# A second level of Strassen's algorithm for two of seven products instead of one, in a two-layer graph kernel

## The chip, the cores and the metric

The kernel runs on one core of one Trainium2 chip. The metric is the device time of one execution in microseconds, as a median of runs. TensorE is called PE in the profile (PEld for its weight loads), VectorE DVE, ScalarE ACT, GpSimd POOL, and the queue of SyncE, which issues most transfers, SP.

## The reference

x is 64 x 256 x 512, the adjacency matrix 256 x 256 of zeros and ones, each weight 512 x 512, all float32.

```python
def layer_0(h, adj, Wq, Wk, Wv):
    q, k, v = h @ Wq.T, h @ Wk.T, h @ Wv.T            # for each of 64 graphs
    rel = adj.T * (q @ k.transpose(0, 2, 1))
    rel = rel / norm(rel, axis=2, keepdims=True)
    return rel @ v

def layer_1(h, adj, weight, bias):
    return (adj @ h) @ weight + bias

x = x + layer_0(maximum(layernorm(x), 0), adj, Wq, Wk, Wv)
x = x + layer_1(maximum(layernorm(x), 0), adj, weight, bias)
```

## The kernel before

**The work of a pair.** Two graphs form a pair, and there are 32 pairs (`NP`). Wq and Wk are merged into one matrix once, so a pair i has three projections of 512 tokens by a 512 x 512 weight: G (h by the merged matrix), V (h by Wv), and the mix (y by the weight of layer 1, added onto x). Between them stand the scores (G with h, then masked, squared, scaled and turned), attend (rel with V, added onto x) and the gather (y, the adjacency with h of layer 1, in two fp32r terms).

**Products.** Each projection, the scores and attend use the Winograd form of Strassen's algorithm: seven products of half-size blocks and sums of blocks. A product of a projection is four matmuls of 128 x 128 weights and 256 columns into one PSUM bank. The factors that are sums come from VectorE: `left_factors` (L168 to L171) and `right_operands` (L133 to L136), each a list of four steps: for the left, s0, the total (in place when it is given three rooms), s1 and s2. The seven factors of a left matrix are then 1: a(0,0), 2: a(0,1), 3: s2, 4: a(1,1), 5: the total, 6: s1, 7: s0. Products are emitted in the order 1, 5, 6, 3, 7, 2, 4; bank_a takes 1, 6, 7 and 4, bank_c 5 and 3, bank_b 2. After each product a `take` reads the bank: ScalarE copies a first block (L431 for G, L475 for V, L514 for the scores), VectorE adds (L433, L477, L516); attend (L619) and the mix (L703) always add on VectorE.

**The second level.** For pairs in the middle, product 2 is dropped and done at a second level: 7 small matmuls of 128 x 128 by 128 columns in four groups, into one bank, bank_d, in the parts at_a, at_b and at_c (L440 for G, L487 for V and mix). Group 1 is small products 1 and 5, group 2 is 6 and 3, group 3 is 7 and 2, group 4 is 4. VectorE adds each part to the result (L449, L491): five adds of 128 columns, one of 256. The small factors on the left come from `second_of_h` and `second_of_y` (four VectorE operations on 128 columns each).

**The order.** PE, DVE and ACT execute in the order in which the program emits (`manual_schedule`). A step list is run by `run_steps`, which after step n emits the other work that a dictionary `side` gives for slot n. So a side item stands on its engine behind the take of its own slot. The function `steady` emits one iteration for 28 values of i: attend of pair i beside V of pair i+1 (`attend_and_v`), scores of i+1, G of i+2, gather of i, mix of i. In it, names stand for lists of single operations:

- `totals`, `row_squares`, `mean`, `root0`, `end0`, `relus0`: LayerNorm of layer 0 by ScalarE, with small VectorE operations (L334 to L354). The result h goes through SP transfers into `blocks` (`place_blocks`, L406, 16 of them) and through VectorE transposes (`turned`, L416), and `sums` are its left factors.
- `halves`, `root`, `end`, `relus`, `uppers`, `lowers`: LayerNorm of layer 1 (L307 to L319, L651, L655); `relus` also emit the bias add on POOL (L647).
- `masks`, `squares`, `norm_root`, `inverse`, `scales`, `place`, `turns`: the scores after their products (L519 to L546); `place` is 16 SP transfers.
- `gs` are G's factors, `y_steps` the left factors of y, `y_second` the small ones; `v_steps` and `rel_steps` are the factors of V and of the turned rel for attend.

The output of a pair is one transfer on POOL's queue (L715), the input one on SP's (L88).

Of the kernel before, what the change touches and what calls it, by code (L numbers as in the profile page):

```python
# [19 lines left out]
def kernel(  # L20
# [35 lines left out]

    nc = tc.nc
    P = 128
# [18 lines left out]
    whole = ctx.enter_context(tc.tile_pool(name="whole", bufs=2))  # L77
# [3 lines left out]
    X, H, HL, G, V, R, H2, Y, HL2, Y2 = ({} for _ in range(10))  # L81
# [22 lines left out]
    warm = const.tile([P, P], F32, name="warm")  # L104
# [39 lines left out]
    def second_right(factor, name):  # L144

        t = const.tile([P, 4, P], F32, name=f"{name}_t")
        return right_operands(lambda j, k: factor[:, j, ts(k, P)], [t[:, n] for n in range(4)])

    def second_left(factor, room):

        return left_factors(lambda i, j: factor[:, j, ts(i, P)], [room[:, n] for n in range(4)])
# [52 lines left out]
    def second_level(matmul, add):  # L204

        bank = ps_m.tile([P, 512], F32, tag="pm", name="bank_d")
        at_a, at_b, at_c = (bank[:, ts(r, P)] for r in range(3))

        def group_1():
            matmul(at_a, 1, True)
            matmul(at_c, 5, False)
            add(0, 0, at_a)
            add(1, 1, at_c)

        def group_2():
            matmul(at_a, 6, False)
            matmul(at_c, 3, False)
            add(0, 1, at_a)  # L220

        def group_3():
            matmul(at_a, 7, False)
            matmul(at_b, 2, False)
            add(1, 1, at_a)
            add(0, None, bank[:, P : 3 * P])

        def group_4():
            matmul(at_a, 4, False)
            add(1, 0, at_a)  # L230

        return group_1, group_2, group_3, group_4

    def two_level_steps(product, take, matmul, add, spacer):

        one, five, six, three, seven, _, four = winograd_steps(product, take)
        groups = second_level(matmul, add)
        return [  # L240
            lambda: run([one]),
            lambda: run([five]),
            lambda: run([six, groups[0]]),
            lambda: run([three, groups[1]]),
            lambda: run([seven, groups[2]]),
            lambda: run([spacer, groups[3]] if spacer else [groups[3]]),
            lambda: run([four]),
        ]
# [76 lines left out]
    def norm_by_scalar(src, scratch):  # L325
# [5 lines left out]
        nb = small.tile([P, TC], F32, tag="nb", name="nb")  # L331

        def total(c):
            nc.scalar.activation(scratch[:, c, :], src[:, c, :], AF.Copy, accum_out=sm[:, c : c + 1])  # L334
# [4 lines left out]
        def square(c):  # L339
            nc.scalar.activation(  # L340
                scratch[:, c, :], src[:, c, :], AF.Square, bias=sm[:, c : c + 1],
                accum_out=sq[:, c : c + 1],
            )
# [9 lines left out]
        def relu(c):  # L353
            nc.scalar.activation(  # L354
                scratch[:, c, :], src[:, c, :], AF.Relu, bias=nb[:, c : c + 1], scale=rs[:, c : c + 1]
            )
# [4 lines left out]
        return each(total), mean, each(square), root, end, each(relu)  # L361
# [12 lines left out]
    def ln0_by_scalar(i):  # L374
        H[i] = work.tile([P, TC, D], F32, tag="hy", name=f"h_{i}")
        return norm_by_scalar(flat(X[i]), H[i])

    def new_ht(i):
        return twice.tile([P, DC, NC, NB * P], F32, tag="ht", name=f"ht_{i}")

    def transposes_by_matmul(i):
        h, ht = H.pop(i), new_ht(i)
        for d in range(DC):
            pt = ps_m.tile([P, T], F32, tag="pm", name="pt")
            for half in range(NC):
                for b in range(NB):
                    nc.tensor.transpose(
                        pt[:, ts(half * NB + b, P)], h[:, b * NC + half, ts(d, P)], ident
                    )
            nc.scalar.copy(ht[:, d].rearrange("p h t -> p (h t)"), pt)  # L390
        HL[i], sums = left_operands(twice, ht, "hs", i)
        return sums

    def second_of_h(i):

        room = work.tile([P, 4, P], F32, tag="hs2", name=f"hs2_{i}")
        HL2[i], steps = second_left(HL[i][2], room)
        return steps
# [11 lines left out]
    def transpose_blocks(i):  # L410

        ht = new_ht(i)
# [7 lines left out]
        HL[i], sums = left_operands(twice, ht, "hs", i)  # L420
        return [(lambda d=d, k=k: step(d, k)) for d in range(DC) for k in range(NC)], sums

    def project_g(i, side={}, second=False, spacer=None):

        g = work.tile([P, DC, NC, HT_], F32, tag="g", name=f"g_{i}")

# [8 lines left out]
        product = product_tokens_moving(HL[i], m_right)  # L435
        if not second:
            winograd(product, take, side)
        else:
            def matmul(out, n, start):
                nc.tensor.matmul(  # L440
                    out, m_second[n], HL2[i][n], start=start, stop=True, skip_group_check=True
                )

            def add(t, k, sums):
                if k is None:
                    dst, sums = g[:, 0:HC, 0, ts(t, P)], sums.rearrange("p (e t) -> p e t", e=HC)
                else:
                    dst = g[:, k, 0, ts(t, P)]
                nc.vector.tensor_add(dst, sums, dst)  # L449

            run_steps(two_level_steps(product, take, matmul, add, spacer), side)
        G[i] = g
# [31 lines left out]
    def second_weights_moving(left, right, x):  # L484

        def matmul(out, n, start):
            nc.tensor.matmul(out, left[n], right[n], start=start, stop=True, skip_group_check=True)  # L487

        def add(b, k, sums):
            dst = x[:, b, 0, 0:HD] if k is None else x[:, b, 0, ts(k, P)]  # L490
# [4 lines left out]
    def v_steps_by_two_levels(i):  # L495
        products = v_products(i)
        second = second_weights_moving(HL2.pop(i), wv_second, V[i])
        return two_level_steps(*products, *second, None)
# [124 lines left out]
    def attend_and_v(i, first_done, v_products, side):  # L623


        for at, (step, v_step) in enumerate(zip(attend_steps(i), v_products)):
            step()
            if at or not first_done:
                v_step()
            run(side.get(at, ()))  # L630


    def ln1(i, exact):
# [9 lines left out]
        def relu_bias(c):  # L643
            if exact:
                whole_h[c] = whole.tile([P, D], F32, tag="h2c", name="h2c")
# [16 lines left out]
    def gather_steps(i, exact):  # L662
# [21 lines left out]
        return [(lambda b=b, d0=d0: step(b, d0)) for b in range(NB) for d0 in range(0, DC, 2)], sums  # L684
# [6 lines left out]
    def second_of_y(i):  # L691

        room = work.tile([P, 4, P], F32, tag="ys2", name=f"ys2_{i}")
        Y2[i], steps = second_left(Y[i][2], room)
        return steps

    def mix(i, side={}, early=False, spacer=None):
        xt = X.pop(i)
        last, taken = i + 1 == NP, set()

        def take(t, k, bank, first):
            block = (slice(None), slice(None), t, slice(k * HD, (k + 1) * HD))
            nc.vector.tensor_add(xt[block], bank.rearrange("p (b e) -> p b e", b=NB), xt[block])  # L703
            if last and ((t, k) in taken or (t, k) == (1, 0)):
                nc.sync.dma_start(out=outs[i][block], in_=xt[block])
            taken.add((t, k))

        product = product_weights_moving(Y.pop(i), w_right)
        if i in Y2:
            second = second_weights_moving(Y2.pop(i), w_second, xt)  # L710
            run_steps(two_level_steps(product, take, *second, spacer), side)
        else:
            winograd(product, take, side, early)
        if not last:
            nc.gpsimd.dma_start(out=outs[i], in_=xt)  # L715
# [94 lines left out]
    m_second, m_second_steps = second_right(m_right[2], "m2")  # L810
    wv_second, wv_second_steps = second_right(wv_right[2], "wv2")
    w_second, w_second_steps = second_right(w_right[2], "w2")
# [8 lines left out]
    def pairs(exact):  # L821
        with tc.manual_schedule(engines=in_order):
            sums = first_pairs(exact)
            v_products = v_steps_by_two_levels(2)
            for i in range(1, NP - 3):
                if i + 4 < NP:
                    load(i + 4)
                sums, v_products = steady(i, exact, sums, v_products, first_done=i > 1)
            last_pairs(exact, sums, v_products)

    def first_pairs(exact):
# [35 lines left out]
            3: turned2[4:6] + relus[2:4], 4: turned2[6:8] + wv_second_steps,  # L867
            5: m_second_steps + turns[0:2], 6: turns[2:4],
# [3 lines left out]
            0: sums2[0:1], 1: sums2[1:2], 2: sums2[2:3], 6: sums2[3:4] + w_second_steps,  # L872
        })
        stats, *parts = ln1(0, exact)
        attend(0, by_slot({c: [stats[c]] for c in range(TC)}, {
# [3 lines left out]
        if exact:  # L879
            nc.vector.tensor_copy(adjt_r, adjt_sb)  # L880
        project_g(2, by_slot(layer_1(parts), {
            1: [inverse], 3: scales + [place], 4: turned3[0:1], 5: turned3[1:2], 6: turned3[2:4],
        }))
        v_steps, rel_steps = attend_operands(1)
        h_second = second_of_h(2)
        y_steps = gather(0, exact, {0: turned3[4:6], 1: turned3[6:7], 2: turned3[7:8]})
        run(y_steps[0:2])
        mix(0, {
# [121 lines left out]
```

## Time and profile before

| | before |
|---|---|
| median of 3 runs | 1717.07 us (1716.89 to 1717.33) |
| the profiled execution, its time | 1717.26 us |
| its span, first to last instruction | 1715.2 us |
| granted TensorE clock | 0.999 |
| PE busy | 1704.2 us, 99% |
| DVE busy | 1386.5 us, 81% |
| ACT busy | 794.5 us, 46% |
| POOL busy | 192.2 us, 11% |

How to read it: busy is the part of the span in which the engine had an instruction under way; matmuls are pipelined, so a busy PE is not one at its peak. VectorE instructions overlap too: one of 512 columns has a duration of 0.68 us, and the next starts 0.60 us after it. The profile counts two instructions for each float32 matmul.

### The profile page before, as it was taken

How to read it: one execution, taken by the hardware profiler on the slowest of the kernel's cores; microseconds unless marked ns; L12 is line 12 of the kernel's file. 1: busy time of each engine (PE TensorE's matmuls, PEld its weight loads, DVE VectorE, ACT ScalarE, POOL GpSimd, SP SyncE). 2: the span in 40 equal slices, each digit the busy share in tenths (PEclk: the TensorE clock that was granted, in tenths of full speed). 3: DMA queues.
4: the chain of work that ended last, by engine and by line, in shares of the span. 5: the costliest groups of instructions: out<-in, count | busy, mean ns of one | idle time of the engine just before them, and what ended most of it. 6: DMA issues, size and time to landing. Idle time of an engine off the chain costs nothing.

```text
span 1715.2 us, 27061 instructions
## 1 busy us (share of the span) xinstructions
PE 1704.2 (99%) x9680; PEld 1523.6 (89%) x9680; DVE 1386.5 (81%) x3141; ACT 794.5 (46%) x1835; POOL 192.2 (11%) x167
## 2 busy tenths in 40 slices
PE   8999999999999999999999999999999999999998
PEld 7989988999898999889998989998899989899986
DVE  6788888888888888888888888888888888788765
ACT  3435544445445455444454354554444544545332
POOL 0011100111101111001111011110011110111111
PEclk9999999999999999999999999999999999999999
DMA  7423332233332233323333322333233333322002
GB/s 239 65 44 70 77 85 68 58 62 79 82 76 73 45 78 76 86 66 61 60 79 81 76 73 42 80 76 84 68 61 62 79 82 74 75 39 58 29 14 75
DMA packets 425984, 122.48 MB, mean 71 GB/s; under 512 B 398064, under 2 KB 399344, under 8 KB 425840
## 3 DMA queue, kind: packets, MB, share of 16 engines
q1 hardware_dynamic: 413248, 80.28, 25.1%
q0 software_dynamic: 8432, 32.51, 5.0%
q10 hardware_dynamic: 4160, 7.87, 1.4%
q8 instruction: 79, 1.29, 0.3%
q14 instruction: 65, 0.53, 0.1%
HBM read 38.27 MB, written 33.55 MB: 42 GB/s over the span
## 4 chain that ended last, share of the span: by engine, by line
PE 97%; DVE 2%; DMA 0%; ACT 0%; issue 0%; ACTq 0%; DVEq 0%
PE bank_a L276 26%; PE bank_c L276 13%; PE bank_a L264 13%; PE py L675 7%; PE bank_a L288 7%; PE bank_c L264 6%; PE bank_d L487 6%; PE bank_a L612 6%; PE bank_c L288 3%; PE bank_c L612 3%; PE bank_d L440 3%; PE bank_b L288 2%; PE bank_b L612 1%; PE bank_b L276 1%; PE pu L577 1%; DVE st L307 0%
## 5 line engine op out<-in xcount | busy, mean ns | idle before, releaser
L475 ACT COPY v<-bank_a 128x512 f32<-128x512 f32 x96 | 56.3, 587 | 459.7 <-PE bank_a L276 459.7
L647 POOL TENSOR_TENSOR x_ring<-x_ring,bias_bc 128x512 f32<-128x512 f32 x128 | 167.3, 1326 | 816.7 <-ACT h2c L319 816.7
L675 PE MATMUL py<-adjt_r,h 128*128 128x256 f32 x1024 | 137.1, 287 | 0.0
L319 ACT ACTIVATE h2c<-x_ring,nb,rs 128x512 f32<-128x512 f32 x128 | 100.6, 810 | 63.8 <-DVE h L655 45.0
L675 PEld LDWEIGHTS py<-adjt_r,h 128*128 128x128 f32 x1024 | 125.8, 189 | 1.6
L276 PE MATMUL bank_a<-w_t,ys 128*128 128x256 f32 x512 | 121.1, 379 | 0.3 <-DVE ys L170 0.3
L264 PE MATMUL bank_a<-hs,m_t 128*128 128x256 f32 x512 | 121.0, 379 | 0.0
L276 PE MATMUL bank_a<-wv_t,hs 128*128 128x256 f32 x512 | 120.9, 379 | 0.0
L703 DVE TENSOR_TENSOR x_ring<-bank_a,x_ring 128x512 f32<-128x512 f32 x128 | 88.5, 691 | 35.1 <-PE bank_a L276 35.1
L276 PEld LDWEIGHTS bank_a<-wv_t,hs 128*128 128x128 f32 x512 | 97.3, 190 | 13.2
L276 PEld LDWEIGHTS bank_a<-w_t,ys 128*128 128x128 f32 x512 | 92.9, 190 | 14.6 <-DVE ys L170 0.7
L264 PEld LDWEIGHTS bank_a<-hs,m_t 128*128 128x128 f32 x512 | 95.1, 190 | 11.8
L715 POOL DMA_DIRECT2D out_dram<-x_ring x31 | 24.0, 773 | 686.4 <-issue 501.2
L307 DVE BATCH_NORM_STATS2 st<-x_ring 128x6 f32<-128x512 f32 x144 | 96.4, 670 | 0.4
L416 DVE STREAM_TRANSPOSE ht<-blocks 128x256 f32<-128x256 f32 x248 | 93.3, 416 | 2.3 <-DMA blocks<-h 2.0
L655 DVE TENSOR_TENSOR h<-h2c,h 128x512 fp32r<-128x512 f32 x128 | 92.3, 723 | 3.0 <-ACT h L651 2.9
L334 ACT ACTIVATE h<-x_ring 128x512 f32<-128x512 f32 x112 | 69.5, 623 | 40.5 <-PE bank_a L276 40.5
L354 ACT ACTIVATE h<-x_ring,nb,rs 128x512 f32<-128x512 f32 x112 | 82.0, 802 | 12.4 <-DVE nb L351 12.4
L679 ACT COPY yt<-py 128x512 f32<-128x512 f32 x128 | 74.5, 582 | 26.1 <-PE py L675 26.1
L536 ACT ACTIVATE rel<-rel,rn 128x256 f32<-128x256 f32 x124 | 52.9, 497 | 68.5 <-DVE rn L533 68.5
L619 DVE TENSOR_TENSOR x_ring<-bank_a,x_ring 128x512 f32<-128x512 f32 x116 | 79.3, 683 | 1.0 <-PE bank_a L612 1.0
L340 ACT ACTIVATE h<-x_ring,sm 128x512 f32<-128x512 f32 x112 | 79.5, 714 | 0.0
(229 smaller groups left out, 4104.2 us busy)
## 6 DMA issues: line engine op xcount, KB each, us to landing
blocks<-h SPq DMA_DIRECT2D x496, 64.0 KB, 2.3
out_dram<-x_ring POOLq DMA_DIRECT2D x31, 1024.0 KB, 4.7
x_ring<-in_x_dram SPq DMA_DIRECT2D x28, 1024.0 KB, 5.2
placed<-rel SPq DMA_DIRECT2D x496, 32.0 KB, 2.0
x_ring<-in_x_dram ACTq DMA_DIRECT2D x4, 1024.0 KB, 5.2
wq_sb<-in_L_gnn_Wq_dram SPq DMA_DIRECT2D x4, 256.0 KB, 5.0
wk_sb<-in_L_gnn_Wk_dram ACTq DMA_DIRECT2D x4, 256.0 KB, 6.2
wv_sb<-in_L_gnn_Wv_dram ACTq DMA_DIRECT2D x1, 1024.0 KB, 5.3
```

What stands on the lines that cost most here:

```text
L264: nc.tensor.matmul(bank[:, e * HT_ : (e + 1) * HT_], right[n][:, d, ts(e, P)], left[n][:, d, :], start=(start and e == 0 and d == 0), stop ...
L276: nc.tensor.matmul(bank[:, b * HD : (b + 1) * HD], left[n][:, d, ts(b, P)], right[n][:, d, :], start=(start and b == 0 and d == 0), stop=( ...
L288: nc.tensor.matmul(bank[:, ts(b, P)], right[n][:, d, ts(b, P)], left[n][:, d, ts(b, P)], start=(start and b == 0 and d == 0), stop=(d == H ...
L307: nc.vector.bn_stats(st[:, c, :], src[:, c, :])
L319: nc.scalar.activation(dst, src[:, c, :], AF.Relu, bias=nb[:, c : c + 1], scale=rs[:, c : c + 1])
L416: nc.vector.transpose(ht[:, d, half].rearrange("p (b n) -> p b n", b=NB), by_half[:, :, half, d])
L487: nc.tensor.matmul(out, left[n], right[n], start=start, stop=True, skip_group_check=True)
L612: nc.tensor.matmul(bank[:, ts(b, HD)], left[n][:, b], right[n][:, b], start=(start and b == 0), stop=True, skip_group_check=True,)
L647: nc.gpsimd.tensor_tensor(xt[:, c, :], xt[:, c, :], bias_bc, ALU.add)
L655: nc.vector.tensor_sub(dst[:, 1, c, :], whole_h[c], dst[:, 0, c, :].bitcast(F32))
L675: nc.tensor.matmul(pm[:, d, :], left[:, b * NC + m, ts(d0 + d, P)], right, start=(n == 0), stop=(n == len(terms) - 1),)
L703: nc.vector.tensor_add(xt[block], bank.rearrange("p (b e) -> p b e", b=NB), xt[block])
```

## The change

Products 2 and 3 of each projection are both dropped and done at a second level. In one small group, the two run side by side: at_a has a bank of its own (bank_e), at_b and at_c share bank_d, and each part is twice as wide, so that one VectorE add serves both. Four pieces change with it:

- The small factors of H (`second_h`) cover both products in operations of 256 columns; those of y are eight operations of 128 columns (k = 2 and k = 3) in the order steps 0 and 1 of both, then steps 2 and 3 of both.
- V of pair i+2 is spread out: its products 1 and 5 stand in G, product 6 in the mix, 7 and 4 and the small groups in the next attend. G's last small group stands in the mix, the mix's in the next attend.
- The LayerNorm sums of pair i+4 stand in the mix (they were those of i+3 in attend), `sums` in G and the gather, and the input load behind attend. The gather's products run half by half.
- The two-level form covers pairs 0 to 31 of the mix and 2 to 31 of G and V, where it covered the middle ones.

The core of the diff:

```diff
-    def second_level(matmul, add):
-        bank = ps_m.tile([P, 512], F32, tag="pm", name="bank_d")
-        at_a, at_b, at_c = (bank[:, ts(r, P)] for r in range(3))
...
+    def two_levels(product, take, matmul, add):
+        bank_a = ps_m.tile([P, 512], F32, tag="pm", name="bank_a")
+        bank_c = ps_m.tile([P, 512], F32, tag="pm", name="bank_c")
+        bank_d = ps_m.tile([P, 512], F32, tag="pm", name="bank_d")
+        bank_e = ps_m.tile([P, 512], F32, tag="pm", name="bank_e")
+        by_k = bank_d.rearrange("p (k s n) -> p k s n", k=2, s=2)
+        at_b, at_c = by_k[:, :, 0], by_k[:, :, 1]
+        at_a = bank_e[:, : 2 * P].rearrange("p (k n) -> p k n", k=2)
+
+        def both(at, n, start=False):
+            for k in range(2):
+                matmul(at[:, k], k + 2, n, start and k == 0)
...
+        def a6():
+            product(bank_a, 6, False)
+            take(0, 1, bank_a, True)
+
+        def c():
+            take(0, 1, bank_c, False)
...
+        def g1():
+            both(at_a, 1, True)
+            both(at_c, 5, True)
+            add(0, 0, at_a)
+            add(1, 1, at_c)
+
+        def g2():
+            both(at_a, 6)
+            both(at_c, 3)
+            add(0, 1, at_a)
+
+        def g3():
+            both(at_a, 7)
+            both(at_b, 2)
             add(1, 1, at_a)
-            add(0, None, bank[:, P : 3 * P])
+            add(0, None, bank_d)
+
+        def g4():
+            both(at_a, 4)
             add(1, 0, at_a)
...
+    def attend_and_v(i, mixed, v, side):
+        one, five, six, three, seven, two, four = attend_steps(i)
+        run_steps([
+            lambda: run([one, mixed["g4"]]),
+            lambda: run([five, v["g1"]]),
+            lambda: run([six, v["a7"]]),
+            lambda: run([three, v["g2"]]),
+            lambda: run([two, v["a4"]]),
+            lambda: run([seven, v["g3"]]),
+            lambda: run([four, v["g4"]]),
+        ], side)
...
+        return steps[0][:2] + steps[1][:2] + steps[0][2:] + steps[1][2:]
...
+    def g_and_v(i, side):
+        g, v = g_by_two_levels(i), v_by_two_levels(i)
+        run_steps([
+            g["a1"], g["c5"], lambda: run([g["a6"], g["g1"]]), v["a1"],
+            lambda: run([g["c"], g["a7"], g["g2"]]), v["c5"], lambda: run([g["a4"], g["g3"]]),
+        ], side)
+        return g, v
+
+    def mix_and_v(i, g, v, side):
+        m = mix_by_two_levels(i)
+        run_steps([
+            m["a1"], m["c5"], lambda: run([m["a6"], m["c"]]), lambda: run([m["g1"], v["a6"]]),
+            lambda: run([m["a7"], m["g2"], g["g4"], v["c"]]), lambda: run([m["a4"], m["g3"]]),
+        ], side)
+        return m
```

The new `steady` (its first lines, which name the lists, are left out):

```diff
+        attend_and_v(i, mixed, v, {
+            0: rel_steps + [root0, end0], 1: relus0[0:2] + gs[0:1], 2: relus0[2:4] + gs[1:2],
+            3: gs[2:3], 4: gs[3:4], 5: halves[0:1], 6: halves[1:2],
+        })
+        if i + 4 < NP:
+            load(i + 4)
         place_blocks(i + 3)
...
         masks, squares, norm_root, inverse, scales, place, turns = scores(i + 1, {
+            0: halves[2:3], 1: halves[3:4] + [root], 2: [end] + relus[0:1], 3: relus[1:2],
+            4: uppers[0:1], 5: uppers[1:2] + h_second[0:2], 6: h_second[2:4],
         })
         turned, sums = transpose_blocks(i + 3)
+        g, v = g_and_v(i + 2, {
             0: masks[0:1] + lowers[0:1] + relus[2:3],
             1: masks[1:2] + lowers[1:2] + relus[3:4],
+            2: uppers[2:4] + squares[0:2],
+            3: lowers[2:3] + squares[2:4] + [norm_root] + turned[0:2],
+            4: lowers[3:4] + [inverse] + scales + [place] + turned[2:4],
+            5: turned[4:7], 6: turned[7:8] + sums[0:1],
+        })
         v_steps, rel_steps = attend_operands(i + 1)
+        y_products, y_steps = gather_steps(i, exact)
+        run_steps(y_products, {
+            0: sums[1:2], 1: sums[2:3], 2: sums[3:4] + y_steps[0:1], 3: v_steps[0:1],
+        })
         y_second = second_of_y(i)
...
+        run(y_steps[1:2])
+        mixed = mix_and_v(i, g, v, {
+            0: y_steps[2:3] + v_steps[1:2] + totals[0:2],
+            1: y_steps[3:4] + y_second[0:2] + totals[2:4],
+            2: y_second[2:8] + mean + row_squares[0:2],
+            3: v_steps[2:4] + row_squares[2:4], 4: turns, 5: rel_steps[0:2],
+        })
+        return norm0, rel_steps[2:4], mixed, v
```

The last mix (pair 31), with its side work:

```diff
+        run_steps([
+            m["a1"], m["c5"], m["g1"], lambda: run([m["a6"], m["c"]]), m["g2"], m["a7"], m["g3"],
+            m["a4"], m["g4"],
+        ], {0: y_steps[2:4] + y_second[0:4], 1: y_second[4:8]})
```

## The prediction

> **What bounds the kernel now.** I read the page's totals first, then the chain that ended last, then one steady pair in the busy times by stretch, the chain and the timeline. The totals and the chain (its shares by engine):
>
> ```profile
> PE 1704.2 (99%) x9680; PEld 1523.6 (89%) x9680; DVE 1386.5 (81%) x3141; ACT 794.5 (46%) x1835; POOL 192.2 (11%) x167
> ...
> PE 97%; DVE 2%; DMA 0%; ACT 0%; issue 0%; ACTq 0%; DVEq 0%
> ```
>
> TensorE carries the chain. VectorE is next, and 81% is a mean over stages. One pair in four stretches (attend with V, scores, G with the first product of y, rest of y with mix), columns PE, PEld, DVE, ACT, POOL:
>
> ```profile
> 754.18:770.69 16.51, 16.51 (x85) 14.40 (x84) 13.03 (x29) 9.70 (x23) 0.77 (x1) 1.00 0.39 131
> 770.69:776.94 6.25, 6.25 (x58) 6.25 (x57) 5.75 (x18) 2.92 (x7) 0.10 (x1) 1.00 0.62 91
> 776.94:790.00 13.06, 13.06 (x73) 11.69 (x72) 11.72 (x26) 9.24 (x24) 5.09 (x4) 1.00 0.24 35
> 790.00:806.57 16.57, 16.57 (x96) 14.86 (x95) 12.89 (x29) 3.36 (x7) 0.00 (x0) 1.00 0.22 33
> ```
>
> VectorE has 9 us spare in 52.4, most of it beside V and mix. Mix as the chain has it:
>
> ```profile
> 743.81 1.73 PE bank_a L276 x8
> 745.54 0.62 PE bank_d L487 x4
> 746.16 1.73 PE bank_c L276 x8
> 747.89 0.45 PE bank_d L487 x4
> ```
>
> A whole product (four matmuls, eight instructions) costs 1.727 us, two small matmuls 0.445, one 0.2225. The first group is 0.175 late. The timeline one pair on shows why, VectorE first, then TensorE:
>
> ```profile
> 797.51 0.29 DVE L168 TENSOR_TENSOR ys<-yt 128x128 f32<-128x128 f32 x1
> 797.71 0.28 DVE L169 TENSOR_TENSOR ys<-yt 128x128 f32<-128x128 f32 x1
> 797.96 0.69 DVE L703 TENSOR_TENSOR x_ring<-bank_a,x_ring 128x512 f32<-128x512 f32 x1
> ...
> 798.05 0.49 PE L487 MATMUL bank_d<-w_t,ys 128*128 128x128 f32 x2
> 798.38 1.89 PE L276 MATMUL bank_c<-w_sb,ys 128*128 128x256 f32 x8
> ```
>
> The factor of small product 5 (L169) ends at 797.99; its matmul would have begun at 797.98, and the next product starts at 798.38. So from VectorE's end to an effective TensorE start is 0.17 us. The same rows give VectorE's other prices, start to start: 0.60 for 512 columns, 0.34 for 256, 0.20 for 128, 0.34 a transpose; 0.10 more where an operation needs its predecessor finished (L133 at 789.96, L134 at 790.68). From a product's end to its take is 0.27 (next product at 796.03, take at 796.30).
>
> **What the Trainium skill says.** "PSUM — Partial Sum Buffer", Engine vs sequencer instructions: VectorE's queue is strictly first in, first out, and matmuls run in program order, though weight loads may run ahead. The rows above agree: the take at 797.96 follows L169 as emitted, and nothing passes the late matmul. The same page, PSUM bank collisions: engines must be kept apart by bank, not address. Agrees: V's fourth group waits 0.41 us (11.8 us over 29) for an add of other columns of bank_d. "VectorE: DVE Perf Modes", The TRN2 errata: a fixed cost per instruction plus the elements; agrees, 256 more columns cost 0.26 us. "GPSIMD Engine Reference", 1. Specifications: POOL contends with VectorE instructions that have two SBUF inputs. Agrees: L170 and L171 on 128 columns take 1.27 and 1.22 us beside POOL's bias adds, 0.28 elsewhere.
>
> **TensorE's arithmetic.** Per steady pair and projection, six products and 7 small matmuls become five and 14: 1.727 - 1.5575 = 0.17 us less, 0.51 for three. Counted: 15 x 1.727 + 42 x 0.2225 + 6.05 (attend) + 6.25 (scores) + 3.72 (y) = 51.27 us, against 51.78 counted and 52.45 measured now (16 pairs from 754.02 to 1593.22). The 0.67 of stalls today (V's last group 0.27, G's 0.19, mix's first 0.175) go: at_a gets a bank to itself, so a fourth group no longer waits for the wide add. The most to win is 1.18 a pair. Outside the 28 steady pairs, 92 projections at two levels save 0.34 each against 85 at 0.17, 16.9 us in all; 14.3 lie in the steady pairs, 2.6 in the ends.
>
> **VectorE's arithmetic.** The five adds at 0.20 and one at 0.34 become five at 0.34 and one at 0.60: +0.96 per projection, 2.9 a pair. Factors of y are 8 operations for 4: +0.8. Factors of H widen to 256: +0.56. Sum 4.2, so 43.4 becomes 47.6 of 51.3. The wide adds on shared banks aren't in the trace; the 128x256 row of L491 gives 0.34, at worst the 512 row's 0.60; a gain is excluded, as the columns double. I take 0.34. Load alone doesn't exceed TensorE, so the order decides. Three chains do, in the new order:
>
> 1. **Mix, first small group (g1).** It follows a6 directly on TensorE. Its last matmul, product 5 of factor 3, needs y_second[3]. That is emitted in slot 2, behind a6's take and c's take. From a6's end: 0.27 + 0.60 + 0.60 + 0.20 (y_second[2]) + 0.10 + 0.28 + 0.17 = 2.22 us. TensorE has only three small matmuls, 0.67. Stall 1.5 us. Queued behind it: V.a6 and the rest of mix.
> 2. **Attend, second product.** Its left factor, rel_steps[1], is last on VectorE after G.g4's add: 0.27 + 0.34 + V.c's take 0.60 + four turns 1.36 + a4's take 0.60 + 0.34 + 0.60 + 0.34 + 0.10 + 0.42 + 0.17 = 5.14. TensorE from G.g4 to there: a4 1.73, g3 0.89, attend's one 0.86, M.g4 0.44 = 3.92. Stall 1.2.
> 3. **Mix, c5.** It needs y_steps[1]. From the end of G.g3: 0.27 + wide add 0.60 + turned 0.34 + sums 0.60 + 0.70 + 0.70 + 0.70 + y_steps[0] 0.60 + v_steps[0] 0.60 + 0.69 + 0.17 = 5.97. TensorE has y 3.72 and a1 1.73 = 5.45. Stall 0.5. Before, the sums of H stood in attend, not here.
>
> Together 3.2 us: period 51.27 + 3.2 = 54.5, 2.05 more than now. Each chain begins where VectorE waits for TensorE, so they add; G has some 4 us of VectorE slack, which clears the lag before the next pair. Bounds: the first is 1.3 to 1.7, the second 0.7 to 1.6, the third 0.1 to 0.9; attend's last product may add 0.15 for the take two steps ahead.
>
> **What else moves.** The ACT sums of LN0 (totals, squares) go from attend to mix, where ACT is busy 3.4 of 16.6 us: nothing; root0 and end0 stay with VectorE in attend. h_second stays under POOL's bias adds, as now; G.g1 needs it 5 us later, so the same 2 us stretch is covered. The outgoing DMA on POOL's queue goes behind M.g4's add, into attend; POOL's next work is the bias adds in scores, over 10 us on. The load on SP now comes after attend, right ahead of the 16 block DMAs (issued over 11.2 us). It waits for that output (4.7 us to land) and takes 5.2; the transposes that need the blocks start one slot later, 14 us behind the first block DMA. I take nothing, at most 0.5 us a pair. The scores' 16 placements keep their slot. The order of y's products only brings the first factor earlier. V's a1 and c5 in G and a6 in mix leave ACT copies with room; all banks but attend's turn around with over 1 us.
>
> **The ends.** -2.6 from the count. The first pair adds some 4 (its mix has w's factors and three more operations on VectorE ahead of a7's take, so a4 waits some 2 us; attend by about 2 more), the last mix 1.0 (there g1 follows c5, and from a1's end VectorE needs 0.27 + take 0.60 + y factors 0.60 and 0.70 + small factors 0.30, 0.20, 0.30, 0.28, with 0.17 to TensorE 3.42, against 1.73 + 0.67 = 2.40). Net +2, from -4 to +8.
>
> **Sum.** The profiled execution took 1717.26 us (span 1715.2, 2.1 around it; the median of the runs is 1717.07, the same within 0.2). 1717.26 + 28 x 2.05 + 2 = 1777.
>
> **The rivals.**
> - *Faster:* TensorE's count decides, and VectorE's chains are shorter than I add them. Price: 28 x 1.18 + 2.6 = 35.6, so 1682; with stalls of 0.5 left, 1696. For it: 99% TensorE, and slack of 9 us. Against: y_second[3] stands behind a take that waits for the very product g1 follows. It decides where the three chains sum to less than 1.18 us. Chance 0.10.
> - *Mix's g1 alone:* chains 2 and 3 are hidden. 28 x (1.5 - 1.18) + 2 = 11, so 1728; with half of them 1752. For it: both have some 0.5 to 1.2 us of margin to gain if transposes or takes run early. Chance 0.20.
> - *VectorE becomes the bound:* the shared-bank adds cost more, POOL stretches more operations, or the blocks land late. 0.1 us more on 15 adds is 1.5 a pair: 1777 + 42 = 1819; a third of it 1791. Chance 0.15.
> - *No change:* the stalls happen to sum to 1.18. 0.02.
>
> The forecast has the remaining 0.53. About 0.2% is what a measurement of this kernel can tell from no change. Slower by more 0.88, within 0.02, faster 0.10. The range leaves out the faster case and the far ends of the others: 1728 to 1808.
>
> **What would show it.** Period 54.5 us (attend to attend) in place of 52.45. Mix's first small group, 0.89 us of work, takes about 2.4 in the chain and waits for a VectorE factor of y; attend's second product waits about 1.2 for the factor of turned; c5 about 0.5. V's fourth group no longer waits. VectorE's busy time rises by about 4 us a pair. A steady period below 52.4 would prove the forecast wrong; one above 55.5 would mean VectorE binds through its load.

## The result, and the profile after

The changed kernel takes **1823.36 us** (median of 4 runs, 1823.32 to 1823.39) against 1717.20 for the kernel before, measured beside it: ratio 1.0618, 95% interval 1.0600 to 1.0637. The forecast was 1777 with a range to 1808. Slower was right, by chains of waits was right, but 46 us were not foreseen.

The page's totals of the kernel after, and the engines' shares of its chain:

```profile
PE 1715.4 (94%) x10274; PEld 1537.6 (84%) x10274; DVE 1504.3 (83%) x3336; ACT 813.0 (45%) x1835; POOL 187.8 (10%) x167
...
PE 65%; DVE 30%; issue 2%; ACT 2%; DMA 0%; DVEq 0%; SPq 0%
```

VectorE's busy time is 118 us more, as counted (4.2 a pair), yet its share of the span is hardly higher, 83% against 81%. What has changed is the chain: TensorE carried 97% of it and carries 65%; VectorE stands in 30%. An engine that is not fuller and yet in the chain is one that is late at certain places.

Where, the busy times by stretch show. One pair, in attend with V, scores, G with V's products 1 and 5, y with mix; columns as before (PE, PEld, DVE, ACT, POOL, then clock and transfers):

```profile
855.58:869.94 14.36, 13.59 (x79) 12.00 (x77) 12.84 (x28) 3.72 (x6) 0.77 (x1) 1.00 0.41 148
869.94:877.07 7.13, 6.52 (x59) 6.33 (x58) 5.42 (x17) 3.75 (x8) 1.75 (x2) 1.00 0.58 83
877.07:891.75 14.68, 14.68 (x82) 13.23 (x81) 10.88 (x24) 9.65 (x24) 3.32 (x3) 1.00 0.23 34
891.75:911.35 19.60, 17.90 (x112) 16.08 (x111) 17.61 (x39) 8.77 (x21) 0.00 (x0) 1.00 0.18 26
```

Work moved between stretches, so they are held against TensorE's count for the new order, not against the old stretches. Attend: 6.05 + V's 7 and 4 3.45 + 16 small matmuls 3.56 = 13.06, measured 14.36, so 1.30 of waits. Scores: 6.25, measured 7.13, 0.88. y and mix: 3.72 + six products 10.36 + 14 small ones 3.12 = 17.20, measured 19.60, 2.40. G: 7 products and 12 small ones are 14.76 by count, and it took 14.68, 0.08 less. Together 4.50: the period is 55.77 (28 pairs from 129.92 to 1691.61) where TensorE's work is 51.27.

The timeline names each wait; TensorE in the same kernel (start, duration, tile; in brackets idle time before, and what ended it):

```profile
842.04 1.96 PE L298 MATMUL bank_c<-w_sb,yt 128*128 128x256 f32 x8 [0.41 <-DVE yt L173]
846.08 0.46 PE L524 MATMUL bank_d<-w_sb,yt 128*128 128x128 f32 x2
847.84 0.49 PE L524 MATMUL bank_d<-w_sb,ys 128*128 128x128 f32 x2 [1.30 <-DVE ys L173]
857.95 1.10 PE L653 MATMUL bank_c<-v,turned 128*128 128x256 f32 x4 [0.77 <-DVE turned L173]
874.28 1.16 PE L310 MATMUL bank_a<-ht,gt 128*128 128x128 f32 x8 [0.61 <-ACT rel L555]
```

The brackets give only the visible part; a wait also shows in the late matmul's longer first instruction. Measured from the end of the work before to the start of the work behind, less the work itself: c5 (the mix's product 5) 0.63, the mix's first small group 1.70, attend's second product 1.15, its last 0.16, and, in the last line, **product 7 of the scores 0.87**. c5, the small group and the second product are the forecast's chains. The wait in the scores is in no step of it. Product 7 takes bank_a after product 6, and waits for ScalarE's copy of that. ScalarE's timeline:

```profile
871.93 0.37 ACT L555 COPY rel<-bank_c 128x256 f32<-128x256 f32 x1 [0.52 <-PE bank_c L310]
873.77 0.20 ACT L334 ACTIVATE rs<-rs 128x4 f32<-128x4 f32 x1 [1.47 <-DVE rs L333]
873.88 0.35 ACT L555 COPY rel<-bank_a 128x256 f32<-128x256 f32 x1
```

and VectorE's beside it:

```profile
873.35 0.18 DVE L330 BATCH_NORM_AGGREGATE mv<-st 128x2 f32<-128x6 f32 x1
873.56 0.17 DVE L333 TENSOR_SCALAR rs<-mv 128x4 f32<-128x4 f32 x1
```

ScalarE does nothing for 1.47 us, and the copy that would empty bank_a stands behind a square root of four columns (L334), which waits for the LayerNorm statistics on VectorE. ScalarE was 45% busy; the copy was late all the same. "TensorE: Matmul & The Clock Gate" of the Trainium skill says in its table at the top (engine queue depth) that ScalarE's queue is strictly first in, first out, and these rows agree. The diff moved `root` from slot 3 of the scores to slot 1, ahead of that copy; it is not among the four pieces that stand under "The change":

```diff
-            0: halves[1:2], 1: halves[2:3], 2: halves[3:4], 3: [root], 4: [end] + relus[0:1],
...
+            0: halves[2:3], 1: halves[3:4] + [root], 2: [end] + relus[0:1], 3: relus[1:2],
```

In the kernel before, ScalarE waited nearly as long for the same statistics, but behind the copy of product 6, and no copy waited with it:

```profile
773.41 0.37 ACT L514 COPY rel<-bank_a 128x256 f32<-128x256 f32 x1 [0.52 <-PE bank_a L288]
775.12 0.20 ACT L312 ACTIVATE rs<-rs 128x4 f32<-128x4 f32 x1 [1.33 <-DVE rs L311]
```

The place alone is not the whole cause; how late the statistics are belongs to it. In the scores of pair 30 the kernel before had `root` in slot 1 already. There it started 3.07 us after the scores did, not 3.83 as here, and product 7 waited 0.1 us.

The 106.1 us by place: 28 periods +91.5, ahead of the first attend +6.9, behind the last one +7.7.

### The profile page after: what moved, and what is told of

Its sections match the earlier page's. It is cut to its first block, busy times and chain, and to the rows that moved or that the text cites. A ratio compares the mean times of both kernels' runs of the same rounds, so it can differ in the third digit from the quotient of the medians.

```text
span 1821.3 us, 28596 instructions
## 1 busy us (share of the span) xinstructions
PE 1715.4 (94%) x10274; PEld 1537.6 (84%) x10274; DVE 1504.3 (83%) x3336; ACT 813.0 (45%) x1835; POOL 187.8 (10%) x167
## 3 DMA queue, kind: packets, MB, share of 16 engines
q8 instruction: 83, 1.36, 0.3%
## 4 chain that ended last, share of the span: by engine, by line
PE 65%; DVE 30%; issue 2%; ACT 2%; DMA 0%; DVEq 0%; SPq 0%
PE bank_a L298 16%; PE bank_a L286 12%; PE bank_c L298 6%; DVE x_ring L757 5%; DVE st L329 4%; PE bank_a L310 4%; PE bank_c L286 3%; PE py L723 3%; PE bank_c L653 3%; PE bank_d L524 3%; PE bank_e L477 3%; PE bank_a L653 3%; PE bank_e L524 2%; DVE x_ring L660 2%; DVE v L533 2%
## 5 line engine op out<-in xcount | busy, mean ns | idle before, releaser
L298 PE MATMUL bank_a<-wv_t,ht 128*128 128x256 f32 x768 | 181.7, 379 | 0.0
L286 PE MATMUL bank_a<-ht,m_t 128*128 128x256 f32 x768 | 181.4, 379 | 0.0
L286 PEld LDWEIGHTS bank_a<-ht,m_t 128*128 128x128 f32 x768 | 145.9, 190 | 19.8
L298 PEld LDWEIGHTS bank_a<-wv_t,ht 128*128 128x128 f32 x768 | 143.5, 190 | 18.3
L363 ACT ACTIVATE blocks<-x_ring,sm 128x512 f32<-128x512 f32 x112 | 80.8, 722 | 153.4 <-DVE sm L360 151.6
L486 DVE TENSOR_TENSOR g<-bank_e,g 128x256 f32<-128x256 f32 x120 | 50.6, 422 | 98.4 <-PE bank_e L477 56.3
L723 PE MATMUL py<-adjt_r,h 128*128 128x256 f32 x1024 | 125.7, 280 | 0.1
L723 PEld LDWEIGHTS py<-adjt_r,h 128*128 128x128 f32 x1024 | 119.9, 188 | 0.3 <-DVE h L703 0.3
L310 PE MATMUL bank_a<-ht,gt 128*128 128x128 f32 x744 | 101.3, 279 | 18.1 <-ACT rel L555 17.7
L310 PEld LDWEIGHTS bank_a<-ht,gt 128*128 128x128 f32 x744 | 90.4, 192 | 23.8 <-ACT rel L555 23.2
L329 DVE BATCH_NORM_STATS2 st<-x_ring 128x6 f32<-128x512 f32 x144 | 97.0, 674 | 0.4
```

The lines of the kernel that those rows point to most:

```text
L286: nc.tensor.matmul(bank[:, e * HT_ : (e + 1) * HT_], right[n][:, d, ts(e, P)], left[n][:, d, :], start=(start and e == 0 and d == 0), stop ...
L298: nc.tensor.matmul(bank[:, b * HD : (b + 1) * HD], left[n][:, d, ts(b, P)], right[n][:, d, :], start=(start and b == 0 and d == 0), stop=( ...
L310: nc.tensor.matmul(bank[:, ts(b, P)], right[n][:, d, ts(b, P)], left[n][:, d, ts(b, P)], start=(start and b == 0 and d == 0), stop=(d == H ...
L329: nc.vector.bn_stats(st[:, c, :], src[:, c, :])
L723: nc.tensor.matmul(pm[:, d, :], left[:, b * NC + m, ts(d0 + d, P)], right, start=(n == 0), stop=(n == len(terms) - 1),)
```

## The experiments

Theory: **order**. Four waits, each at one place in an in-order queue, make the loss; VectorE's load doesn't. Rival: **load**. VectorE has 4.2 us a pair more to do, and what is taken from one wait comes back as the next. Ratios are against the kernel before, with their 95% intervals.

**One wait at a time.** V's product 6 put ahead of the mix's first small group:

```diff
-            ... lambda: run([m["g1"], v["a6"]]),
+            ... lambda: run([v["a6"], m["g1"]]),
```

> V's product 6 goes ahead of mix's first small group; nothing else changes. Order theory: the group then has 1.73 us more until it needs y_second[3] (ready 2.2 us after a6's end, needed after 2.4), so the stall of 1.70 us a pair goes: 29 mixes, 49 us less, about 1775. Load theory (VectorE's work in y, mix and attend sets the pace): VectorE does the same work, so the wait comes back in the next stages; within 10 us of 1823.

Measured 1784.70 us, ratio 1.0391 (1.0374 to 1.0409): 38.7 less. The wait of 1.70 is gone and 0.3 of it comes back further on: product 4 of the mix now waits 0.41, counted as above, and attend's second product 0.11 less. Timeline, VectorE's take of product 7 and TensorE's product 4:

```profile
996.96 0.69 DVE L757 TENSOR_TENSOR x_ring<-bank_a,x_ring 128x512 f32<-128x512 f32 x1
```

```profile
996.95 0.61 PE L477 MATMUL bank_e<-ht,m_t 128*128 128x128 f32 x4
997.70 1.99 PE L298 MATMUL bank_a<-w_t,yt 128*128 128x256 f32 x8
```

The two small matmuls of 996.95 end at 997.39; product 4 starts at 997.70, when the take has emptied bank_a. Without the stall, VectorE no longer waits anywhere in the mix behind c5's take, so it is as late at product 7 as its list is long.

The root of LayerNorm behind the scores' third copy instead of ahead of it, in the pairs of the middle and in pair 30:

```diff
-            0: halves[2:3], 1: halves[3:4] + [root], 2: [end] + relus[0:1], 3: relus[1:2],
+            0: halves[2:3], 1: halves[3:4], 2: [root], 3: [end] + relus[0:2],
```

> In the scores the square root of layer 1's LayerNorm moves from slot 1 to slot 2 and what follows it to slot 3, so that it stands behind product 6's copy on ScalarE. Order theory: the stall of 0.87 us before product 7 goes in 29 pairs, 24 us less, about 1799. Load theory: VectorE's statistics are as late as before, so the scores wait elsewhere; within 8 us of 1823.

Measured 1799.82, ratio 1.0473 (1.0455 to 1.0490): 23.5 less. A period in the middle falls from 55.74 to 54.87 us, by the 0.87 of the wait. An instruction of 0.2 us one slot later, with what follows it, is worth 23.5 us. This is the wait that the forecast lacked.

The transposes of the turned rel one slot earlier, ahead of the adds of G's last group:

```diff
-            3: v_steps[2:4] + row_squares[2:4], 4: turns, 5: rel_steps[0:2],
+            3: v_steps[2:4] + row_squares[2:4] + turns, 5: rel_steps[0:2],
```

> The four turns move from slot 4 of the mix to slot 3, ahead of a7's take, where VectorE waits 0.92 us and then 0.32 us for TensorE. Order theory: attend's second product waits 1.14 us less 0.1 to 0.2, in 28 pairs 27 us less, about 1796. Load theory predicts a gain too, as idle time is used, but at most 1.2 us a pair and only if nothing behind it is late: 0 to 34 us.

Measured 1810.21, ratio 1.0537 (1.0520 to 1.0555): 13 less, half of what was expected. Attend's second product, and the take of mix's product 4 on VectorE:

```profile
1017.66 1.10 PE L653 MATMUL bank_c<-v,turned 128*128 128x256 f32 x4 [0.40 <-DVE turned L173]
```

```profile
1015.10 0.69 DVE L757 TENSOR_TENSOR x_ring<-bank_a,x_ring 128x512 f32<-128x512 f32 x1 [0.72 <-PE bank_a L298]
```

The chain had a second start. With the transposes out of the way, VectorE waits 0.72 us for product 4 itself, and from that product's end to the second product the take, two adds and two factors need 2.84 us where TensorE has 2.2. A wait that is taken away leaves the next one that ends nearly as late.

The first factor of V for attend out of the way of y's factors, for chain 3:

```diff
-            ... 2: sums[3:4] + y_steps[0:1], 3: v_steps[0:1],
+            ... 2: sums[3:4] + y_steps[0:1],
...
-            0: y_steps[2:3] + v_steps[1:2] + totals[0:2],
+            0: y_steps[2:3] + v_steps[0:2] + totals[0:2],
```

> One factor of V (0.60 us of VectorE) moves from ahead of y_steps[1] to behind it. Order theory: c5's stall of 0.63 goes, but c5's take comes some 0.2 later and the first small group with it: 0.4 us x 28 = 12 us less, about 1811. Load theory: 0, 1823.

A miss: 1849.87, ratio 1.0786 (1.0756 to 1.0815), 26.5 more where 12 less was expected. c5's wait fell to 0.25, but the factor, now behind the mix's first take, delays the takes that the first small group waits for, and that wait grew to 2.26 us; an ordinary period came to 55.88. The rest is TensorE's clock, which in the profiled execution fell in 11 of the 28 periods. Timeline and busy times of one of them, cut where the trace's record of the clock changes (PEclk is the third number from the end):

```profile
1026.46 0.49 PE L524 MATMUL bank_d<-w_sb,ys 128*128 128x128 f32 x2 [1.30 <-DVE ys L173]
1026.78 3.10 PE L298 MATMUL bank_a<-wv_t,ht 128*128 128x256 f32 x8
```

```profile
1023.90:1027.31 3.41, 1.92 (x11) 1.40 (x10) 3.24 (x11) 0.00 (x0) 0.00 (x0) 1.00 0.06 10
1027.31:1030.72 3.41, 3.41 (x10) 2.67 (x9) 2.18 (x6) 2.43 (x6) 0.00 (x0) 0.50 0.02 5
1030.72:1034.14 3.42, 3.42 (x24) 3.16 (x23) 1.70 (x4) 1.31 (x4) 0.00 (x0) 1.00 0.00 0
```

From 1023.63 to 1026.78 TensorE did 0.89 us of work in 3.15; then the clock was 0.50 for 3.41 us, a product took 3.10 instead of 1.89, and that period 57.6.

**Order against load.** The same two transposes repeated, 0.68 us of VectorE work a pair, once where VectorE idles in G and once in the chain to c5:

```diff
-            5: turned[4:7], 6: turned[7:8] + sums[0:1],
+            5: turned[4:7] + turned[4:6], 6: turned[7:8] + sums[0:1],               # in the idle place
+            5: turned[4:7], 6: turned[7:8] + turned[4:6] + sums[0:1],               # in the chain
```

> Two of the eight transposes of H are done a second time, in slot 5 of G, where VectorE waits 1.45 us for TensorE: 0.69 us more VectorE work a pair. Order theory: nothing waits for it, 0 within 4 us of 1823. Load theory: 0.69 x 28 = 19 us more, 1842.

> The same two transposes stand one slot later, behind the adds of G's third group, on the chain that ends at c5. Both theories: c5's stall of 0.63 becomes 1.3, 0.69 x 28 = 19 us more, 1842; more than that if TensorE's clock drops after longer pauses.

In the idle place 1825.69, ratio 1.0626 (1.0609 to 1.0644), not told apart from the 1.0618 without it; a period in the middle is 55.74 us with and without. In the chain 1842.33, ratio 1.0731 (1.0713 to 1.0749): 19 more, which is 28 x 0.68. Equal load, and here the place alone decides: VectorE's load as such does not set the pace of the kernel as changed.

**All orders mended.** Both swaps that worked, and four more of the kind: V's take of `c` goes into attend, all transposes and two sums of H into G's slot 5, two factors of V into the gather, two factors of rel directly behind the turns:

```diff
-            lambda: run([two, v["a4"]]),
+            lambda: run([two, v["a4"], v["c"]]),
...
-            lambda: run([m["a7"], m["g2"], g["g4"], v["c"]]), lambda: run([m["a4"], m["g3"]]),
+            lambda: run([m["a7"], m["g2"], g["g4"]]), lambda: run([m["a4"], m["g3"]]),
...
-            5: turned[4:7], 6: turned[7:8] + sums[0:1],
+            5: turned[4:8] + sums[0:2],
...
-            0: sums[1:2], 1: sums[2:3], 2: sums[3:4] + y_steps[0:1], 3: v_steps[0:1],
+            0: sums[2:3], 1: sums[3:4], 2: y_steps[0:1], 3: v_steps[0:2],
...
-            0: y_steps[2:3] + v_steps[1:2] + totals[0:2],
+            0: y_steps[2:3] + totals[0:2],
...
-            3: v_steps[2:4] + row_squares[2:4], 4: turns, 5: rel_steps[0:2],
+            3: v_steps[2:4] + row_squares[2:4], 4: turns + rel_steps[0:2],
```

> VectorE and TensorE do what the changed kernel does, in another order: V's product 6 ahead of mix's first group, the LayerNorm root in the scores' slot 2, V.c's take in attend's slot 4, the last transpose of H and two of its sums in G's slot 5, a second factor of V in the gather, rel_steps[0:2] behind the turns. Order theory: c5 and the first group no longer wait, attend's second product waits at most 0.2, M.g4 0.2, attend's last product 0.16; period 51.9, so 1823 - 28 x 3.85 = 1715, below the kernel before by 0 to 5. Load theory: VectorE's 47.6 us a pair can't be packed that tightly; period 53 or more, over 1745.

Measured 1725.89, ratio 1.0049 (1.0032 to 1.0066): 97.5 of the 106 us come back with every instruction kept, but 11 us less than expected. The next kernel is the same with y's small factors of pair 29 made beside the last scores:

```diff
+        y_second = second_of_y(a, "hs2")
         masks, squares, norm_root, inverse, rn, turn_at_once = scores(
-            c, {0: [v["g4"]]}, by_matmul=True
+            c, {0: [v["g4"]], 1: y_second[0:4], 2: y_second[4:8]}, by_matmul=True
         )
...
-            1: masks[0:1], 2: masks[1:2] + squares[0:2], 3: squares[2:4] + y_second,
+            1: masks[0:1], 2: masks[1:2] + squares[0:2], 3: squares[2:4],
```

> As the reordered kernel, and the small factors of y of pair 29 are made beside the scores of pair 31 instead of in the attend ahead of mix 29. Order theory: the a6 of that mix waits 1.9 us less, 2 us less than the reordered kernel. Load theory: no difference that can be measured.

1723.88, ratio 1.0038 (1.0024 to 1.0052), 2.0 less, as expected. The 11 us are waits that were hidden behind the four: a period is 52.27. Timeline of TensorE:

```profile
964.98 1.99 PE L298 MATMUL bank_a<-w_t,yt 128*128 128x256 f32 x8
...
967.70 1.03 PE L653 MATMUL bank_a<-v,turned 128*128 128x256 f32 x4
968.82 0.49 PE L524 MATMUL bank_e<-w_t,yt 128*128 128x128 f32 x2
969.14 0.39 PE L524 MATMUL bank_e<-w_t,ys 128*128 128x128 f32 x2
969.37 1.03 PE L653 MATMUL bank_c<-v,turned 128*128 128x256 f32 x4
```

Product 4 could start at 964.67 and starts 0.31 later, behind the take of product 7; by the start of the work behind it, it loses 0.41. From attend's first product (967.70) to its second (969.37) it is 1.67 us, where the work is 1.31: the mix's last group between them waits 0.36 for bank_e. The next kernels go after these waits, each with the edits of the one before.

V's third factor into the mix's slot 0, where VectorE had 0.56 us idle:

```diff
-            0: y_steps[2:3] + totals[0:2],
+            0: y_steps[2:3] + v_steps[2:3] + totals[0:2],
...
-            3: v_steps[2:4] + row_squares[2:4], 4: turns + rel_steps[0:2],
+            3: v_steps[3:4] + row_squares[2:4], 4: turns + rel_steps[0:2],
```

> The kernel with six edits (1723.88 us), and the third factor of V for attend is made behind the mix's first take, where VectorE waits 0.56 us for the next product, instead of ahead of the take of product 7. Order theory: the take of product 7 and all behind it stand 0.60 us earlier on VectorE, so product 4 of the mix no longer waits for its bank (0.31 a pair) and the mix's last group in attend no longer waits for the add of bank_e (0.3 a pair, or 0.26); 28 x 0.57 to 0.61 = 16 to 17 us: 1707, below the kernel before. Load theory: VectorE executes as many instructions and has no idle time in the mix, so what is taken out of one wait comes back as another: 1720 or more.

1717.67, ratio 0.9998 (0.9990 to 1.0007): 6.2 less instead of 17. The wait of product 4 is gone, but that of the mix's last group grew from 0.36 to 0.52: its chain starts at G's last group, and that start is TensorE's own. So the gain is 0.41 - 0.16 = 0.25 a pair. Then attend's product 7 right behind product 2:

```diff
-            lambda: run([two, v["a4"], v["c"]]), lambda: run([seven, v["g3"]]), lambda: run([four, v["g4"]]),
+            two, lambda: run([seven, v["a4"], v["c"]]), lambda: run([v["g3"], four, v["g4"]]),
```

> As the one with V's third factor earlier, and in attend the products stand two, seven, V's 4, V's group 3, four, in place of two, V's 4, seven, group 3, four. Product 4 of attend takes the bank of product 7 after 2.6 us of other work instead of 0.9, and its wait of 0.1 to 0.16 us a pair goes: 28 x 0.11 = 3, so 3 us below the other. If the take of V's 4 or the LayerNorm sums behind it then come late for the scores, nothing, or up to 5 us more.

**1713.68, ratio 0.9973 (0.9963 to 0.9984)**: 4 less, and 0.3% faster than the kernel before. Its attend and its mix by stretch:

```profile
962.09:975.68 13.59, 13.34 (x79) 11.78 (x77) 13.21 (x30) 3.72 (x6) 0.77 (x1) 1.00 0.42 154
...
996.62:1013.95 17.33, 17.33 (x112) 15.89 (x110) 15.90 (x37) 8.77 (x21) 0.00 (x0) 1.00 0.20 30
```

The stretch of y and mix is 2.3 us shorter than in the changed kernel and within 0.13 of TensorE's count. The period is 51.9. In attend, 0.53 above its count, VectorE is busy for 13.21 of 13.59 us. The next kernel asks whether this rest is VectorE's load; in it the mix's last group stands behind attend's second product:

```diff
-            lambda: run([one, mixed["g4"]]), lambda: run([five, v["g1"]]), lambda: run([six, v["a7"]]),
+            one, lambda: run([five, mixed["g4"]]), lambda: run([v["a7"], v["g1"], six]),
```

> As the one with attend's product 7 earlier (1713.68 us), and at the start of attend the products stand one, five, mix's group 4, V's 7, V's group 1, six in place of one, mix's group 4, five, V's group 1, six, V's 7. There the mix's last group still waits 0.41 us a pair for the add that empties bank_e, which stands on VectorE behind the takes of mix's product 4: from the end of G's last group VectorE needs 0.27 for the first add, four turns, two factors, the take and the add, which is longer than TensorE's work up to that group. With attend's second product in front, the bank has 0.87 us more. Order theory: 28 x 0.41 = 11 us less, 1702; if attend's second product then waits for its own factor or product 6 for its bank, up to 0.2 a pair is given back, 1708. Load theory: the same 1714, since VectorE's work is the same.

1713.72, ratio 0.9973 (0.9962 to 0.9984): nothing. The group no longer waits, and V's last group does, at the other end of attend. TensorE, and VectorE's last work ahead of that group:

```profile
974.48 1.03 PE L653 MATMUL bank_a<-blocks,turned 128*128 128x256 f32 x4
975.73 0.71 PE L524 MATMUL bank_e<-wv_t,ht 128*128 128x128 f32 x4 [0.21 <-DVE v L533]
```

```profile
974.46 0.68 DVE L329 BATCH_NORM_STATS2 st<-x_ring 128x6 f32<-128x512 f32 x1
975.18 0.18 DVE L330 BATCH_NORM_AGGREGATE mv<-st 128x2 f32<-128x6 f32 x1
975.28 0.39 DVE L533 TENSOR_TENSOR v<-bank_e,v 128x256 f32<-128x256 f32 x1
```

It could start at 975.35. VectorE runs from the take of mix's product 4 at 962.89 to here with one pause of 0.27 us, and what was taken from one wait came back as the next, as the load theory says. Yet load is not shown to be the cause. The last add, which empties bank_e for V's group, stands behind statistics of the next LayerNorm (L329, L330), and no product of attend needs those. Behind the add they would let it start some 0.8 us earlier, by these rows. No run moves them, so whether the rest of attend is order or load stays open.

The last one changes an end of the kernel at 1713.68: y's small factors ahead of the LayerNorm steps in the mix of pair 30, where GpSimd's bias adds run beside them.

```diff
-            0: [root, end, y_steps[3]] + relus[0:2], 1: uppers[0:2] + y_second[0:4],
-            2: y_second[4:8] + lowers[0:1] + relus[2:3], 3: lowers[1:2] + relus[3:4],
+            0: [y_steps[3]] + y_second[0:4] + [root, end] + relus[0:2],
+            1: y_second[4:8] + uppers[0:2], 2: lowers[0:1] + relus[2:3], 3: lowers[1:2] + relus[3:4],
```

> As the one with attend's product 7 earlier, and in the mix of the pair before the last the small factors of y are emitted ahead of the LayerNorm's steps and so ahead of GpSimd's bias adds. Two of them took 1.32 and 1.24 us in place of 0.28 there, and the first small group waited 2.08 us. 2 us below the other; 0 if the factors then run beside the bias adds as before.

A miss: 1715.54, ratio 0.9985 (0.9979 to 0.9992), 1.9 more. VectorE, and TensorE's product 7:

```profile
1678.85 1.38 DVE L174 TENSOR_TENSOR ys<-ys 128x128 f32<-128x128 f32 x1
1680.26 1.24 DVE L175 TENSOR_TENSOR ys<-ys,ys 128x128 f32<-128x128 f32 x1
```

```profile
1682.15 3.68 PE L298 MATMUL bank_a<-w_t,ys 128*128 128x256 f32 x8 [3.79 <-DVE x_ring L757]
```

The first group no longer waits. But the bias adds now meet the other two factors, which have moved ahead of product 6's take, so product 7 waits 3.79 us for its bank, and the clock falls behind that.

## Why the prediction was wrong, point by point

- **TensorE's count: right.** 51.27 us a pair; the stretch of G, without waits, took 14.68 where the count is 14.76, and the mended orders come down to 51.9.
- **VectorE's count: right.** +4.2 a pair, 1386.5 to 1504.3; the wide adds on a shared bank follow one another in 0.33, as taken. V's group behind the wide add no longer waits.
- **Chain 1 (1.5): 1.70.** From product 6's end to the last small matmul 2.37 us instead of 2.22. The two takes follow each other in 0.72 and not 0.60: both add onto the same block of x, so the second needs the first finished. The forecast had that price (0.10) and didn't put it on this pair.
- **Chain 2 (1.2): 1.15**, and attend's last product 0.16 where it said "may add 0.15". Right, but the 0.16 was left out of the sum: 4.5 us.
- **Chain 3 (0.5): 0.63**, inside its bounds.
- **"Three chains do, in the new order": the step that failed.** There was a fourth, in the scores. The forecast followed VectorE's queue for each consumer. What it says of ScalarE ("nothing" for the LayerNorm sums, "leave ACT copies with room") asks how much ScalarE has to do and not what stands ahead of a copy. So it did not cost the move of `root` from slot 3 to slot 1, and this term was left at nothing. 0.87 x 28 = 24 us; taking it away gave 23.5, and at 1799.82 us the kernel lies inside the stated range.
- **The ends (+2, from -4 to +8): +14.6.** Of this 6.9 lie ahead of the first attend and 7.7 behind the last. They can't be held one by one against the forecast's 4 and 1.0, because three products of V (5.2 us) now stand ahead of the first attend. The first mix waits at three places (1.04, 1.36 and 0.41 us) and the first attend at two (0.35 and 1.37). In the last pairs y's eight small factors stood ahead of a take for pair 29 (product 6 waits 1.77; moving them gave 2.0 us back), and for pair 30 two of them ran beside bias adds, 1.31 and 1.23 us instead of 0.28, with 2.08 us of waiting. The forecast named only the last mix.
- **The sum.** 46.4 us too little: 24.4 the scores, 4.5 attend's last product, 9.2 chains 1 and 3, 12.6 the ends; 1.4 less for chain 2, and 1.6 less because the period before is 52.51 over all 28 pairs where the forecast took 52.45 from 16. That is 47.7. The forecast's own rounding (54.47 to 54.5 a pair, 1776.7 to 1777) takes off 1.2, and the rest is within the reading.
- **The rivals.** "Faster" failed for the reason that it gave against itself, and "mix's g1 alone" because chains 2 and 3 cost 1.15 and 0.63. "VectorE becomes the bound" was to be told by a period above 55.5; the period is 55.77, and yet equal work in an idle place cost nothing and 97.5 us came back by order alone. That test could not tell load from one more wait.

## What to carry to other kernels

For each instruction that a change moves, write down for every in-order queue that it enters, the half-empty ones too, what stands behind it and who waits for that: an instruction of 0.2 us that waits for another engine holds up everything behind it, whatever the engine's load. A wait that is taken away gives only the distance to the next releaser, so look for the second start of the chain before giving a gain. Where an engine runs through a stretch without a pause, ask which of its work only a later stretch needs, before calling it full. A test for "load" must add work at an idle place: a longer period alone doesn't tell.

## What the runs showed of the hardware that was not expected

Waits cost more than their length when they cluster, and not always. Behind the same pauses, to within 0.01 us, the clock held in the kernel at 1723.88 us and fell in the one at 1713.68. Busy times of the mix of pair 30, the former first (PEclk is the third number from the end):

```profile
1686.00:1690.00 4.00, 1.92 (x11) 1.40 (x10) 3.93 (x6) 1.97 (x4) 2.53 (x2) 1.00 0.01 2
1690.00:1694.00 4.00, 3.17 (x17) 2.41 (x16) 3.90 (x11) 0.99 (x2) 0.55 (x1) 1.00 0.00 0
```

```profile
1676.00:1680.00 4.00, 1.92 (x11) 1.41 (x10) 3.93 (x6) 1.97 (x4) 2.54 (x2) 1.00 0.00 0
1680.00:1684.00 4.00, 3.89 (x14) 2.97 (x14) 3.90 (x11) 0.99 (x2) 0.55 (x1) 0.64 0.00 0
```

"TensorE: Matmul & The Clock Gate" of the Trainium skill, Part 1, says that the clock goes to half after an idle window of about 3.4 us. Here the measurement decides: TensorE was not idle for a window. It worked 1.92 of 4 us ahead of this fall, and 1.92 of 3.41 ahead of the one in the experiment on chain 3.

The traces' records of the clock show that it also matters when a pause falls. In the experiment on chain 3 the long pause stands in every pair of the middle, and the clock fell in 11 of the 28, the first time at 235.42 us and the last at 1706.56. These falls lie whole numbers of 3.413 us apart (431 of them from the first to the last), and each lasts 3.41 us at half the clock, as the busy times there show. In every other trace in which the clock changes more than once, the changes keep this distance too, but stand elsewhere in the execution. So in these runs a pause cost more than its length where it filled enough of one such stretch. Each fall costs some 1.7 us (half of 3.413): two products there took 3.10 and 2.41 instead of 1.89 each, and the period 57.6 instead of 55.9. How little work is enough for a fall, the runs don't settle. In these stretches, one with 1.77 us of work was followed by the full clock (the kernel at 1723.88 us), and one with 1.82 by half (the one at 1713.68).
